# Three steps of a state-space layer's hand-written round moved to other places in the round

## The chip, the cores and the metric

The kernel runs on one core of a Trainium2 chip. A core has a matrix engine (TensorE, PE in the profile, with its weight loads shown apart as PEld), a vector engine (VectorE, DVE), an activation engine (ScalarE, ACT), a general engine (GpSimd, POOL) and DMA queues issued by SyncE (SP) and others. Each engine takes its own instructions in the order in which they stand in its queue, and waits on semaphores for the others. The metric is the device time of one execution in microseconds (us), lower is better; the median over several runs is compared.

## The reference

The whole kernel is a four-layer decoder stack of twelve sublayers on a tensor x of 32 sequences of 128 tokens with 128 features. Each sublayer is `x = x + f(layernorm(x))`. Only the first sublayer, a state-space layer, is touched here:

```
zxbcdt = x @ in_proj_w.T                 # z (256), xBC (512), dt (32)
xBC = silu(causal conv of width 4 over the tokens, + conv_b)
dt = 0.001 + 0.099 * sigmoid(dt_raw + dt_bias);  dA = dt * -exp(A_log)
Yd, Yo = products in chunks of 64 tokens, weighted by exp of sums of dA
y = (Yd + Yo + D_skip * x_ssm) * silu(z)
y = y * rsqrt(mean(y*y) + 1e-5) * norm_w
out = layernorm(y @ out_proj_w.T) * ln_w + ln_b
```

The result is added to the normalized input, and that sum to x.

## The kernel before

The 32 sequences are 8 groups (G = 8) of 4 sequences (J = 4). `layer0` walks through 34 rounds, n = -2 to 31; round n belongs to group i = n // 4 and to place j = n % 4 in it, and computes the chunk products of sequence j of group i. Around that core each round carries pieces of other groups' work, so that the engines have something to do while one product waits for the next. These pieces are generators: `go(what, g)` runs group g's next piece, up to its next `yield`. For TensorE, ScalarE and VectorE the order in which the program issues instructions is kept exactly (`follow(T, A, V)`, line 914; line 194 is the recording helper, so nearly every instruction bears that line in the profile). GpSimd's and SyncE's queues are ordered by the framework's scheduler.

The pieces that matter:

- `entry(g)`, line 753, the group's layer norm, four pieces. 1: statistics on VectorE and a power on GpSimd. 2: one small VectorE operation for the shift (`sh`, tile `s`). 3: four ScalarE activations that write `xn`. 4: GpSimd adds `xn` to x (line 758); TensorE transposes `xn` into a PSUM tile, and ScalarE copies that into `xnT`, which all projections of the group read.
- `decays(g)`, line 762, the step sizes, five pieces. 1: four small matmuls of `xnT` and a VectorE addition that writes `dts`. 2: a ScalarE tanh. 3: six VectorE operations, `dA` among them. 4: a matmul of `dA` (lines 784 and 785) and a ScalarE exponential. 5: one VectorE multiplication (line 788). The result is first read when `first` begins on that group's sequence 0.
- `gate(g, b)`, line 720, two pieces. 1: a matmul of `xnT`, a ScalarE copy to `z`, and a ScalarE tanh. 2: a VectorE operation on `z`.
- `conv(g, c)`, line 700, five pieces: projection and copy; the first tap on ScalarE (`gmid<-bmid,w`); three taps on VectorE; tanh; a VectorE product. One block c is done in each round, in the round's own group + 1 for j = 0 and 1, and + 2 for j = 2 and 3, so that round 2 is the first to read the newest `xnT`.
- `joined(g)`, line 864, the output: piece 1 is VectorE work (skip term, product with z); 2 two ScalarE squares; 3 the output projection `op`, a sum of squares `msp` and a ScalarE copy; 4 statistics, which read `msp` first; 5 two small VectorE operations; 6 four ScalarE activations; 7 GpSimd sums.
- `first(n)` prepares a sequence two rounds ahead (five matmuls, two transposes, three ScalarE reads of PSUM, three GpSimd products); `second`, `exponentials` and `weighted` make the decay weights one round ahead; `third(n)` does the 128 small matmuls of the chunk products and then two VectorE reads of PSUM (`gmid<-ps`).

All small PSUM tiles come from one pool of two buffers (`ps`, line 219). A tile can be written only when the readers of the tile before the last one are done. So the order of the steps also sets who waits for whose reader.

Of the kernel before, what the change touches and what calls it, by code (L numbers as in the profile page):

```python
# [204 lines left out]
def program(ctx, tc, cols, x, ctxt, mask, drop, dfirst, dsmall, dwide, drows, dunits, dexperts, dconst, drel, dwq, out):  # L205
# [466 lines left out]
    def layer0(lead):  # L672
# [119 lines left out]
        def first(n):  # L792

            i, j = n // J, n % J
            side, B, C = sides[i % 2], convs[i, 2], convs[i, 3]
            dt, dte = dts[i]
            xt, xd, xe, right = xts[n % 2], xds[n % 3], xes[n % 3], rights[n % 2]

            p = ps((128, 320))
            left, edge = (side[:, j, k].rearrange("p r c -> p (r c)") for k in range(2))  # L800
            mm(p[:, 256:320], edge, W0["fold64"])
            mm(p[:, 128:256], left, W0["upper64"])
            mm(p[:, 64:128], B[:, j, :], C[:, j, 64:128])
            for ch in range(2):
                at = slice(64 * ch, 64 * ch + 64)
                mm(p[at, 0:64], B[:, j, at], C[:, j, at])
            cbl = sm.tile([128, 384], F32, tag="cbl", name="cbl", bufs=CBLS)
            A.copy(cbl[:, 0:320], p)
            A.activation(cbl[:, 320:384], p[:, 256:320], AF.Exp)
            P.tensor_tensor(right, bc(cbl[:, 256:320], 1, 8), bc(W0["hm24"], 2, 64), ALU.mult)  # L810
            p = ps((128, 256))
            for c in range(2):
                turn_over(p[:, c * 128 : (c + 1) * 128], convs[i, c][:, j, :])
            A.copy(xt, p)
            P.tensor_tensor(diagonal(xd), xt.rearrange("p (a n e) -> p a n e", a=8, n=4),
                            bc(dt[:, j, :].rearrange("p (a n) -> p a n", a=8), 3, 8), ALU.mult)
            P.tensor_tensor(xe.rearrange("p (h e) -> p h e", e=8), xt[0:64].rearrange("p (h e) -> p h e", e=8),
                            bc(dte[0:64, j, :], 2, 8), ALU.mult)
            fronts[n] = xd, xe, cbl, right

        def second(n):

            _, _, cbl, right = fronts[n]
            segs = [two((128, 2, 8, 64)) for _ in range(2)]
            for r in range(4):
                mm(segs[r // 2][:, r % 2], identb, bc(acausal, 1, 8), True, False)
            for r in range(4):
                rows = slice(32 * r, 32 * r + 24)
                mm(segs[r // 2][:, r % 2], cbl[rows, 128:256], right[rows], False, True)
            mids[n] = bbig((128, 2, 16, 64)), segs  # L830

        def exponentials(n):
            m, segs = mids[n]
            for h in range(2):
                A.activation(m[:, h], segs[h].rearrange("p r a q -> p (r a) q"), AF.Exp)

        def weighted(n, h):

            m = mids[n][0]
            V.tensor_tensor(m[:, h], m[:, h], bc(fronts[n][2][:, 0:64], 1, 16), ALU.mult)  # L840

        def third(n):

            i, j = n // J, n % J
            (xd, xe, cbl, _), m = fronts.pop(n), mids.pop(n)[0].rearrange("p s h q -> p (s h) q")
            if j == 0:
                sums[i] = [acc((128, 2, J, 64)) for _ in range(2)]
                offs[i] = gmid((128, 2, J, 64))
            for b in range(2):
                for k in range(4):  # L850
                    for r in range(4):
                        for ch in range(2):
                            rows = slice(64 * ch, 64 * ch + 64)
                            mm(sums[i][ch][32 * r : 32 * r + 32, b, j], flat(xd[rows, 4 * b + r, k]), m[rows, 16 * b + 4 * r + k],
                               k == 0, k == 3)
            p = ps((128, 2, 2, 64))
            for b in range(2):
                mm(p[:, 0, b], xe[:, 128 * b : 128 * b + 128], cbl[0:64, 64:128])
            for b in range(2):
                mm(p[:, 1, b], K["spread"][:, 128 * b : 128 * b + 128], cbl[:, 320:384])  # L860
            V.tensor_copy(offs[i][:, :, j], p[:, 0])
            V.tensor_tensor(offs[i][:, :, j], offs[i][:, :, j], p[:, 1], ALU.mult)
# [43 lines left out]
        def go(what, g, *more):  # L906

            if 0 <= g < G:
                key = what, g, *more
                if key not in late:  # L910
                    late[key] = what(g, *more)
                next(late[key], None)
# [36 lines left out]
        for n in range(-2, G * J):  # L949
            i, j = n // J, n % J  # L950

            g, c = (i + 1, j) if j < 2 else (i + 2, j)
            go(conv, g, c)
            if 0 <= n + 2 < G * J:
                first(n + 2)
            go(conv, g, c)
            if j == 0:
                go(joined, i - 1)
                go(gate, i, 0)
            elif j == 1:  # L960
                go(joined, i - 1)
            elif j == 2:
                go(decays, i + 2)
                go(decays, i + 2)
            elif j == 3:
                go(decays, i + 2)
                go(gate, i + 1, 1)
                go(entry, i + 3)
            if 0 <= n + 1 < G * J:
                second(n + 1)  # L970
            go(conv, g, c)
            if 0 <= n + 1 < G * J:
                exponentials(n + 1)
                weighted(n + 1, 0)
            if 0 <= n < G * J:
                third(n)
            if 0 <= n + 1 < G * J:
                weighted(n + 1, 1)
            go(conv, g, c)
            if j == 0:  # L980
                go(joined, i - 1)
                go(joined, i - 1)
            elif j == 1:
                go(joined, i - 1)
                go(joined, i - 1)
                go(joined, i - 1)
                go(entry, i + 2)
            elif j == 2:
                go(decays, i + 2)
                go(decays, i + 2)  # L990
                go(gate, i + 1, 1)
            elif j == 3:
                go(entry, i + 3)
                go(entry, i + 3)
                go(gate, i + 1, 0)
            go(conv, g, c)
            if n >= G * J - 5:
                next(lead)
# [997 lines left out]
    SY.dma_start(out=wq8, in_=dwq)  # L1996
    lead1, run1 = layer1()
    rest0 = layer0(lead1)
    load_units(5)
    lead2, run2 = layer2()  # L2000
# [45 lines left out]
```

## Time and profile before

| | |
|---|---|
| median of 3 runs | 3010.7 us (3003.21, 3010.7, 3012.12) |
| the profiled execution | 2999.27 us, span 2997.5 us |
| share of the span: PE, PEld, DVE, ACT, POOL | 85%, 55%, 70%, 51%, 33% |
| the state-space layer | about the first 430 us of the span |
| steady group of four rounds (178.77 to 230.62) | 51.85 us, of them DVE busy 37.01, PE 41.49, ACT 26.88 |
| mean granted TensorE clock in that group | 0.84 of full |

A row of the timeline gives start and duration in us, the engine, the line, the operation with the tile written and the tiles read, and how many instructions were merged; in brackets stands how long the engine sat idle before it and which engine's work ended that idle time. A row of the waits gives the waiting engine and its tile, the releasing engine, the total us, the number of waits and the longest.

### The profile page before, as it was taken

How to read it: one execution, taken by the hardware profiler on the slowest of the kernel's cores; microseconds unless marked ns; L12 is line 12 of the kernel's file. 1: busy time of each engine (PE TensorE's matmuls, PEld its weight loads, DVE VectorE, ACT ScalarE, POOL GpSimd, SP SyncE). 2: the span in 40 equal slices, each digit the busy share in tenths (PEclk: the TensorE clock that was granted, in tenths of full speed). 3: DMA queues.
4: the chain of work that ended last, by engine and by line, in shares of the span. 5: the costliest groups of instructions: out<-in, count | busy, mean ns of one | idle time of the engine just before them, and what ended most of it. 6: DMA issues, size and time to landing. Idle time of an engine off the chain costs nothing. (4 is left out here: it accounts for less than half of the span.)

```text
span 2997.5 us, 55783 instructions
## 1 busy us (share of the span) xinstructions
PE 2554.4 (85%) x22535; PEld 1638.7 (55%) x22554; DVE 2093.0 (70%) x4263; ACT 1527.0 (51%) x3540; POOL 1003.2 (33%) x1033
## 2 busy tenths in 40 slices
PE   5788889999989989999998999988876989876564
PEld 3555567777744445566664444445553767544343
DVE  5777667888888756677786554468895339867873
ACT  4555445444412255666664444467772226555563
POOL 3333352232310123335451000124334365324544
PEclk8888889999999999999998999989997989997776
DMA  3000000000000000000000000000003253100000
GB/s 112 2 2 2 5 20 8 5 8 1 12 11 1 0 33 2 5 9 9 12 2 15 1 1 1 1 1 2 2 2 131 85 179 109 40 18 11 22 11 22
DMA packets 50147, 68.36 MB, mean 23 GB/s; under 512 B 3681, under 2 KB 41570, under 8 KB 49762
## 3 DMA queue, kind: packets, MB, share of 16 engines
q1 hardware_dynamic: 42608, 33.84, 3.7%
q0 software_dynamic: 6848, 27.81, 2.8%
q8 instruction: 178, 2.92, 0.4%
q10 hardware_dynamic: 434, 3.14, 0.3%
q14 instruction: 79, 0.65, 0.1%
HBM read 51.11 MB, written 13.68 MB: 22 GB/s over the span
## 5 line engine op out<-in xcount | busy, mean ns | idle before, releaser
L194 PE MATMUL ps<-cs,bbig 128*128 128x128 f32 x2208 | 328.5, 289 | 88.9 <-ACT bbig L194 34.9
L194 PEld LDWEIGHTS ps<-cs,bbig 128*128 128x128 f32 x2208 | 253.9, 146 | 192.4 <-ACT bbig L194 85.9
L194 ACT COPY bbig<-ps 128x512 f32<-128x512 f32 x418 | 228.9, 590 | 238.9 <-PE ps L194 238.9
L194 DVE TENSOR_REDUCE s<-two 128x8 f32<-128x1024 f32 (+1 forms) x192 | 234.1, 1220 | 119.6 <-PE two L194 118.3
L194 DVE TENSOR_TENSOR bbig<-bbig 128x256 f32<-128x256 f32 (+4 forms) x394 | 272.8, 742 | 18.6 <-ACT bbig L194 17.1
L194 PE MATMUL two<-xnT,u 128*128 128x512 f32 x512 | 260.8, 610 | 11.8 <-ACT bmid L194 6.3
L194 PE MATMUL acc<-bmid,u 128*128 128x512 f32 x448 | 239.4, 621 | 26.8 <-DVE bmid L194 25.2
L194 PE MATMUL two<-gbig,gmid 32*128 32x512 f32 (+1 forms) x1248 | 217.1, 570 | 2.4 <-ACT bbig L194 2.4
L194 DVE TENSOR_TENSOR bmid<-bmid,ps 128x512 f32<-128x512 f32 x192 | 130.2, 684 | 111.5 <-ACT bmid L194 91.8
L481 POOL TENSOR_SCALAR gbig<-bmid,cs 128x512 f32<-128x512 f32 x96 | 148.6, 1564 | 160.9 <-ACT bmid L194 160.9
L194 ACT ACTIVATE bbig<-two,s 128x256 f32<-128x256 f32 (+1 forms) x512 | 189.7, 419 | 20.2 <-DVE s L194 16.8
L194 ACT ACTIVATE bbig<-bbig 128x512 f32<-128x512 f32 (+1 forms) x160 | 128.1, 801 | 87.0 <-DVE bbig L194 86.6
L194 PE MATMUL ps<-cs,xn 128*128 128x128 f32 x288 | 68.9, 321 | 105.8 <-ACT xn L194 80.5
L194 ACT ACTIVATE bmid<-two 128x512 f32<-128x512 f32 x104 | 62.0, 597 | 190.5 <-PE two L194 182.1
L194 PEld LDWEIGHTS two<-xnT,u 128*128 128x128 f32 x512 | 92.2, 192 | 115.7 <-issue 55.8
L194 PEld LDWEIGHTS acc<-bmid,u 128*128 128x128 f32 x448 | 81.9, 197 | 128.9 <-DVE bmid L194 73.2
L194 ACT ACTIVATE bmid<-two,ws 128x512 f32<-128x512 f32 x128 | 85.1, 686 | 112.1 <-PE two L194 111.9
L194 ACT ACTIVATE bbig<-bbig,s 128x128 f32<-128x128 f32 x384 | 118.7, 387 | 27.1 <-DVE s L194 27.1
L1070 POOL TENSOR_TENSOR bbig<-bbig,s 128x1024 f32<-128x1024 f32 x32 | 60.6, 1892 | 214.1 <-PE two L194 152.6
L194 DVE TENSOR_TENSOR bbig<-two,s 128x1024 f32<-128x1024 f32 (+1 forms) x128 | 122.6, 958 | 8.6
L493 POOL MEMSET val<- 128x512 f32 x72 | 39.3, 549 | 257.3 <-PE acc L194 256.1
L194 PE MATMUL two<-xT,we 128*128 128x256 f32 x448 | 109.8, 400 | 8.6 <-ACT xT L194 4.2
(307 smaller groups left out, 5930.6 us busy)
## 6 DMA issues: line engine op xcount, KB each, us to landing
u<-in_units SPq DMA_DIRECT2D x10, 768.0 KB, 4.3
gmid<-in_ctx SPq DMA_DIRECT2D x16, 256.0 KB, 2.9
xs<-bbig SPq DMA_DIRECT2D x4, 903.0 KB, 5.7
xt<-xs SPq DMA_DIRECT2D x28, 129.0 KB, 2.3
x<-in_x SPq DMA_DIRECT2D x8, 256.0 KB, 7.2
gmid<-in_mask SPq DMA_DIRECT2D x8, 256.0 KB, 3.1
ys<-bbig SPq DMA_DIRECT2D x2, 1024.0 KB, 6.2
gmid<-ys SPq DMA_DIRECT2D x8, 256.0 KB, 3.9
```

What stands on the lines that cost most here:

```text
L194: d = f(*args, **kwargs)
L481: P.tensor_scalar(o[:, n, :], k, K["n4"][:, n : n + 1], None, ALU.mult)
L493: P.memset(o, 0.0)
L1070: (V if c2 else P).tensor_tensor(pr[:, four, :], pr[:, four, :], bc(nm[:, four], 2, 256), ALU.mult)
```

## The change

Three things move in the rounds; no operation is added or removed.

- The fourth piece of the norm, `entry(i + 2)` with the transposes, goes from the end of round j = 1 to the end of round j = 0.
- The fourth and fifth piece of `decays` each go later: the fourth (matmul of `dA`, exponential) from the end of round 2 to the end of round 3, the fifth (the multiplication) from the start of round 3 to the start of the next group's round 0, where it stands ahead of the first piece of `joined`.
- At the end of round 3, `gate(i + 1, 0)` goes ahead of the second and third piece of `entry(i + 3)`, and the moved piece of `decays` stands behind all of them.

```
             if j == 0:
+                go(decays, i + 1)
                 go(joined, i - 1)
                 go(gate, i, 0)
...
             elif j == 3:
-                go(decays, i + 2)
                 go(gate, i + 1, 1)
                 go(entry, i + 3)
...
             if j == 0:
                 go(joined, i - 1)
                 go(joined, i - 1)
+                go(entry, i + 2)
             elif j == 1:
                 go(joined, i - 1)
                 go(joined, i - 1)
                 go(joined, i - 1)
-                go(entry, i + 2)
             elif j == 2:
-                go(decays, i + 2)
                 go(decays, i + 2)
                 go(gate, i + 1, 1)
             elif j == 3:
+                go(gate, i + 1, 0)
                 go(entry, i + 3)
                 go(entry, i + 3)
-                go(gate, i + 1, 0)
+                go(decays, i + 2)
             go(conv, g, c)
```

In the built program GpSimd's and SyncE's instructions stand in the same order as before; those of TensorE, ScalarE and VectorE are moved as the diff says.

More of the change, by code (lines that the diff above doesn't have):

```diff
@@ L957, in layer0 @@
             if j == 0:
+                go(decays, i + 1)
                 go(joined, i - 1)
@@ L965, in layer0 @@
             elif j == 3:
-                go(decays, i + 2)
                 go(gate, i + 1, 1)
@@ L982, in layer0 @@
                 go(joined, i - 1)
+                go(entry, i + 2)
             elif j == 1:
@@ L986, in layer0 @@
                 go(joined, i - 1)
-                go(entry, i + 2)
             elif j == 2:
-                go(decays, i + 2)
                 go(decays, i + 2)
@@ L992, in layer0 @@
             elif j == 3:
+                go(gate, i + 1, 0)
                 go(entry, i + 3)
                 go(entry, i + 3)
-                go(gate, i + 1, 0)
+                go(decays, i + 2)
             go(conv, g, c)
```

## The prediction, made before the changed kernel was run

> **What bounds the kernel now.** I read the busy shares first (no engine is full in the first 430 us, where the changed layer runs), then the waits between 30 and 372 us, then the timeline of one group. The waits show which hand-overs cost VectorE and TensorE time:
>
> ```profile
> DVE dts L194 <- PE ps L194: 41.6, 7, 7.9
> ...
> PE ps L194 <- ACT xnT L194: 22.3, 5, 4.6
> PE ps L194 <- DVE dA L194: 21.7, 8, 4.2
> ...
> DVE z L194 <- ACT bmid L194: 14.7, 8, 2.4
> ACT xn L194 <- DVE s L194: 12.5, 6, 2.2
> ```
>
> All five touch moved steps. In the group that I take as the pattern (i = 3) they stand so:
>
> ```profile
> 222.95 1.65 ACT L194 ACTIVATE bmid<-bmid,s 128x128 f32<-128x128 f32 x4 [2.38 <-DVE s L194]
> 224.51 0.56 ACT L194 COPY xnT<-ps 128x512 f32<-128x512 f32 x1
> ...
> 225.12 2.08 PE L194 MATMUL ps<-xnT,w 128*128 128x512 f32 x2 [4.63 <-ACT xnT L194]
> ...
> 227.23 0.58 ACT L194 COPY bmid<-ps 128x512 f32<-128x512 f32 x1 [2.16 <-PE ps L194]
> ...
> 228.83 0.43 ACT L194 COPY cbl<-ps 128x320 f32<-128x320 f32 x1 [1.01 <-PE ps L194]
> ...
> 230.62 0.29 DVE L194 TENSOR_TENSOR dts<-ps,ww 128x128 f32<-128x128 f32 x1 [7.10 <-PE ps L194]
> ...
> 236.74 0.22 DVE L194 TENSOR_SCALAR dts<-dts 128x128 f32<-128x128 f32 x1
> ...
> 237.43 0.66 PE L194 MATMUL ps<-dA,w 64*64 64x128 f32 x2 [2.40 <-DVE dA L194]
> ...
> 241.41 0.69 DVE L194 SCALAR_TENSOR_TENSOR z<-bmid,z 128x512 f32<-128x512 f32 x1 [2.44 <-ACT bmid L194]
> ...
> 244.89 2.92 DVE L194 SCALAR_TENSOR_TENSOR gmid<-bmid,w,gmid 128x508 f32<-128x508 f32 x3 [1.53 <-ACT gmid L194]
> ```
>
> Round 2 begins with a chain: ScalarE's `joined` activations, then the `xnT` copy, then TensorE's projection, ScalarE's copies, the step-size matmuls; VectorE sits 7.10 us until `dts`. Round 3 has another: TensorE stands 2.40 us at `dA`, with the gate's and the convolution's matmuls behind it, so the gate's `z` comes late for VectorE (2.44) and then the convolution's taps (1.53). The end of round 3 and the start of round 0 read differently:
>
> ```profile
> 199.05 0.69 DVE L194 SCALAR_TENSOR_TENSOR gmid<-bmid,gmid 128x512 f32<-128x512 f32 x1
> 199.17 1.65 ACT L194 ACTIVATE xn<-x,s 128x128 f32<-128x128 f32 x4 [2.18 <-DVE s L194]
> 199.65 1.65 DVE L194 SCALAR_TENSOR_TENSOR bmid<-gmid,w,acc 128x256 f32<-128x256 f32 x4
> 200.72 0.56 ACT L194 COPY z<-ps 128x512 f32<-128x512 f32 x1
> ```
>
> From 199.65 to 213.0 VectorE has no gap: round 0 is VectorE's.
>
> **The norm's transposes, a round sooner.** Round 2: `xnT` is ready, so the projection follows `third` at 220.0 instead of 225.12. The step that ends last is then ScalarE's: its four `joined` activations still end at 224.60 (they wait for VectorE's `s`). Its copy follows at once, 224.6 to 225.2, and the `cbl` copy at 225.2 instead of 228.83. From there the old spacing holds (step sizes on VectorE 1.8 us after the `cbl` copy): 227.0 instead of 230.62, 3.6 us. Against that, VectorE's taps now fall under GpSimd's sums of `joined` (224.68 to 227.28) and its products; such taps took 2.92 to 3.10 us where 2.54 stood here, so 3.2 are left. Groups 1 to 5 have this; group 0, with no `joined` before it, waited 2.22 instead of 7.10 and gains 1.2. Sum 1.2 + 5 x 3.2 = 17.2.
>
> TensorE still has one idle stretch there: `first`'s transposes need the PSUM buffer that ScalarE's copy frees at 225.2, and all before them is done by 222.4, so 2.8 us. The row for such a stretch is the matmul of `dA`: after 2.40 us it took 0.66 (half rate) in groups -1, 3 and 5 and 0.40 in four others. [...] By the row it is three times in seven, and the price then is that of group 5, where the step-size matmuls took 1.92 instead of 1.08 us: with the transposes 1.1 us on the path. The rule gives 17.2, all cold 11.7; I go by the row: 3/7 x 1.1 x 5 = 2.4 less, 15.
>
> Round 0, where the transposes go: four matmuls, 0.61 us, behind `msp`, and ScalarE's 0.56 us copy. Round 1's projection stands behind them (its buffer was `msp`'s), and with it `first`, the taps and VectorE, which already waits 1.60 us for the taps there. So 0.65 us of loss in six groups, 3.9. GpSimd's addition at line 758 keeps its place, and no DMA moves.
>
> **The products of the step sizes, a round later.** Round 3: TensorE is done with round 2's `third` at 235.04 and goes straight to the gate (1.1 us), ScalarE's copy and tanh of `z` follow by 237.4, the convolution's projection at 236.2, its copy at 237.4, and the tap on ScalarE ends 3.2 us after VectorE's step-size operations begin. VectorE itself needs from their start 2.06 us to the gate's product and 2.1 us for that and the statistics: its taps can start at 4.16 us. Before, they started after 7.69, 7.11, 5.57, 7.00, 8.15, 5.57 and 7.12 us (groups -1 to 5; the last has no statistics, so 3.2 after). Sum 48.2 - (6 x 4.16 + 3.2) = 20.0 if TensorE runs at full rate; at half rate the gate's and the convolution's matmuls take 2.0 instead of 1.1 each and `first` 0.8 more, so the taps start at about 5.5 everywhere, and 48.2 - 38.5 = 9.7 is the gain. Three sevenths of the way from the first: 15.6.
>
> **The same products, where they go.** The `dA` matmul finds its buffer free when VectorE has read `third`'s tile, a wait (0.47 us) that round 0's projection has today. Then the exponential stands behind the norm's four activations (end 200.82): 201.1. `first`'s matmuls, behind it by the buffer, start at 201.15 instead of 201.34. But VectorE's multiplication now stands at the head of round 0, ahead of `joined`, and cannot start before 201.1; queued behind it are all of round 0's VectorE operations, and for these wait ScalarE's squares and TensorE's `msp`. `joined` starts at 201.4 instead of 199.65: 1.75 us, the multiplication's 0.28 included. Part may come back, because GpSimd's two sums (200.89 to 203.57) then run beside the four operations that read PSUM and not beside those with two SBUF inputs. [...] That gives back up to 1.0, so 0.75. I take 1.3 between the two. If TensorE is at half rate, the gate's matmul takes 2.0, the norm's activations slip to 199.85, and it is 2.4. It counts where `joined` and a norm meet, groups 1 to 5: 6.5 (3.75 to 12).
>
> **The gate ahead of the norm.** ScalarE copies and squashes `z` in the 2.18 us that it waits for `s` (1.2 us of work, matmul done at 197.6), so nothing. Without that cover it would delay `xn`, which is the 2.4 above.
>
> **The sum.** 15 + 15.6 - 3.9 - 6.5 = 20 us. Worst ends together: 11.7 + 9.7 - 3.9 - 12 = 5.5; best: 17.2 + 20.0 - 3.9 - 3.75 = 29.5. What follows the layer is in the same queues and starts that much sooner. Against the profiled execution, 2999.3 (span 2997.5 and 1.8 around it), this is 2979. The median shown stands 11.4 above it; I subtract from the median: 3010.7 - 20 = 2991 (2981 to 3005).
>
> **The rivals.** A: the VectorE wait at the head of round 0 takes back most of what rounds 2 and 3 give, with TensorE at half rate: the worst ends, 3005. For it: three of seven `dA` rows were at half rate. Against: it needs all of them.
>
> B, slower: the half rate spreads. Round 2 took 6.12 us from `dts` to the step-size operations at full rate, 8.64 in group 5 and 7.58 in group 2; round 3's taps came 2.6 us later cold. So a cold round costs about 2.5 us, and it was cold in seven of the thirteen such rounds. The change cuts TensorE's stretches into other lengths, and one of 2 to 3 us stays in each group. From eight more cold rounds among the 28 the 20 us are gone; sixteen more give 3010.7 - 20 + 40 = 3031. Against: the longest stretch, 4.63 us, is removed, and the mean clock should rise.
>
> C: the waits are exchanged without gain, since something else ends each group, within 9 us: 3006. Against: VectorE is busy 37.01 of 51.85 us, and the gaps removed are its own.
>
> **Chances.** Forecast 0.70, A 0.13 (0.04 of it still a gain above 0.3%), B 0.12, C 0.05. A measurement of this kernel tells about 0.3%, 9 us, from no change. Faster 0.70 + 0.04 = 0.74, same 0.09 + 0.05 = 0.14, slower 0.12. The range runs from the best end, 2980, to 3014, leaving out B and a little below.
>
> **What would show it.** In the changed profile the wait of PE for `xnT` is gone (it was 22.3), DVE's for `dts` falls from 41.6 to about 22 (5 x 3.6 + 1.2 less), PE's for `dA` from 21.7 to near the prologue's 4; DVE's for `z` vanishes; a new wait of DVE for ACT `dts`, about 1.4 us each in five groups, appears, and PE waits for `xnT` again at most briefly, in round 1. A steady group takes about 47.5 instead of 51.5 us. I am wrong if a group's granted clock falls under 0.8, or if the new wait is above 5 us.

## The result, and the profile after

| | before | changed |
|---|---|---|
| median of 12 runs each | 3010.64 us (3003.21 to 3025.06) | 2985.33 us (2978.25 to 3006.37) |
| ratio of the two | | 0.9925, 95% interval 0.9906 to 0.9944 |
| the profiled execution, its span | 2999.27, 2997.5 us | 2981.45, 2979.7 us |
| start of `joined` in groups 1 to 6 | 97.7 to 354.7 us | 97.3 to 334.6 us |
| the group i = 3: length, TensorE's granted clock | 51.55 us, 0.83 | 47.64 us, 0.86 |

The changed kernel is faster, by 22.6 us if the ratio is taken of 3010.64, and by 17.8 between the two profiled executions. In the traces the layer alone gives 20.1 us by the start of group 6's `joined`; 2.3 us of that are lost again by the end of the span. The twelve executions of the changed kernel differ in TensorE's granted clock: over the whole span it was 0.924 in the fastest (2978.25 us), and 0.915, 0.914 and 0.912 in the three slowest (2992.62, 3000.57 and 3006.37 us).

The waits between 30 and 360 us of the changed kernel (total us, number of waits and longest):

```profile
DVE dts L194 <- PE ps L194: 22.8, 7, 4.1
...
PE ps L194 <- ACT bmid L194: 20.6, 12, 3.0
...
PE ps L194 <- DVE gmid L194: 15.5, 14, 1.9
...
PE ps L194 <- ACT dts L194: 8.2, 6, 1.5
...
DVE dts L194 <- ACT dts L194: 7.6, 6, 1.3
...
ACT xn L194 <- DVE s L194: 5.7, 6, 1.0
...
PE ps L194 <- DVE dA L194: 4.2, 1, 4.2
```

VectorE's wait for `dts` is halved (it was 41.6). TensorE's for `dA` (21.7) is down to the prologue's one, TensorE's for `xnT` (22.3) and VectorE's for `z` (14.7) are not in the list any more. In their place TensorE waits for ScalarE's `bmid` copy (20.6, where it was 8.9), and VectorE for ScalarE's `dts` at the head of round 0 (7.6).

Round 2 of group i = 3 in the timeline of the changed kernel (start, duration, engine, operation, and in brackets the idle time before it):

```profile
215.75 1.65 ACT L194 ACTIVATE bmid<-bmid,s 128x128 f32<-128x128 f32 x4 [2.38 <-DVE s L194]
217.31 0.56 ACT L194 COPY bmid<-ps 128x512 f32<-128x512 f32 x1
...
217.77 0.42 ACT L194 COPY cbl<-ps 128x320 f32<-128x320 f32 x1
...
217.92 0.44 PE L194 MATMUL ps<-cs,gmid 128*128 128x128 f32 x2 [2.35 <-ACT bmid L194]
...
218.36 1.88 PE L194 MATMUL ps<-w,xnT 128*128 128x32 f32 x8
...
220.34 0.29 DVE L194 TENSOR_TENSOR dts<-ps,ww 128x128 f32<-128x128 f32 x1 [4.02 <-PE ps L194]
...
220.55 3.14 DVE L194 SCALAR_TENSOR_TENSOR gmid<-bmid,w,gmid 128x508 f32<-128x508 f32 x3
```

VectorE's wait for `dts` is 4.02 us where it was 7.10. TensorE's idle stretch before `first`'s transposes is 2.35 us, and the step-size matmuls behind it take 1.88 us: the half rate. The end of round 3 and the head of round 0:

```profile
237.44 0.40 PE L194 MATMUL ps<-dA,w 64*64 64x128 f32 x2 [1.86 <-DVE gmid L194]
...
238.54 1.65 ACT L194 ACTIVATE xn<-x,s 128x128 f32<-128x128 f32 x4 [1.04 <-DVE s L194]
240.10 0.26 ACT L194 ACTIVATE dts<-ps 64x128 f32<-64x128 f32 x1
...
240.27 1.27 POOL L758 TENSOR_TENSOR x<-x,xn 128x512 f32<-128x512 f32 x1 [5.30 <-ACT xn L194]
240.38 1.30 DVE L194 TENSOR_TENSOR dts<-dts 64x128 f32<-64x128 f32 x1 [1.27 <-ACT dts L194]
...
241.61 1.64 DVE L194 SCALAR_TENSOR_TENSOR bmid<-gmid,w,acc 128x256 f32<-128x256 f32 x4
```

The new wait is 1.27 us, and the multiplication behind it takes 1.30 us beside GpSimd's addition (L758), where it took 0.28 before.

To see where the 20 us came from, I cut each group at VectorE's own marks: the start of `joined`, round 0's taps, the reading of `msp`, round 1's taps, the `dts` addition, `dA`, round 3's taps, the next `joined`. Sums over groups 1 to 5, from the timelines, in us:

| from, to | before | changed | gain |
|---|---|---|---|
| `joined` to round 0's taps | 38.23 | 28.93 | 9.3 |
| round 0's taps over `msp` to round 1's taps | 48.47 | 53.77 | -5.3 |
| round 1's taps to `dts` | 70.90 | 52.31 | 18.6 |
| `dts` to `dA` | 35.84 | 42.02 | -6.2 |
| `dA` to round 3's taps | 32.15 | 20.74 | 11.4 |
| round 3's taps to the next `joined` | 31.46 | 39.49 | -8.0 |
| sum | 257.05 | 237.26 | 19.8 |

### The profile page after: what moved, and what is told of

It reads as the page before. It is cut to its first block, busy times and chain, and to the rows that moved or that the text cites. A ratio compares the mean times of both kernels' runs of the same rounds, so it can differ in the third digit from the quotient of the medians.

```text
span 2979.7 us, 55782 instructions
## 1 busy us (share of the span) xinstructions
PE 2551.2 (86%) x22535; PEld 1632.4 (55%) x22554; DVE 2095.4 (70%) x4263; ACT 1525.5 (51%) x3540; POOL 1008.7 (34%) x1033
## 5 line engine op out<-in xcount | busy, mean ns | idle before, releaser
L194 PE MATMUL two<-xT,we 128*128 128x256 f32 x448 | 108.3, 396 | 10.7 <-DMA we<-in_experts,wrow 5.9
```

Source lines behind the costliest of these rows:

```text
L194: d = f(*args, **kwargs)
```

## The experiments

The theory is that of the prediction: three separate chains, each with its own gain, whose sum is the result. The rivals are that the wait at the head of round 0 takes back a large part (A), and that TensorE's half rate decides (B). Runs sent together share a chip and the runs of the kernel before; ratios are to the kernel before on the same chip, with 95% intervals. "Step" below is 3.413 us, the grid on which TensorE's granted clock changes in these traces; the last section shows it.

**Each part alone, on the kernel before.** The norm's transposes alone:

```diff
             if j == 0:
...
                 go(joined, i - 1)
+                go(entry, i + 2)
             elif j == 1:
...
-                go(entry, i + 2)
```

> The kernel before, with the norm's transposes alone moved a round sooner. The sum on record has this at 15.0 - 3.9 = 11 us faster (about 3000). The reading of the changed trace says otherwise: round 2 starts its step sizes 3.2 us sooner, but the wait of 2.35 us before the two transposes puts TensorE at half rate, so that the step-size operations come 8.2 instead of 6.1 us after it, and round 1 loses 0.5: 5 x (3.2 - 2.2 - 0.5) + about 1 = 3 to 4 us faster at most, within 9 us of before. A group's stretch from dts to the step-size operations shows which: 6.1 us or 8.2 us.

Measured: 0.9979 (0.9965 to 0.9992), 6 us. Round 2's gain is there (round 1's taps to `dts` 10.7 us instead of 13.86), but `dts` to `dA` takes 8.5 instead of 6.37, `dA` to round 3's taps takes 7.9 to 8.0 in every group, and all groups are 50.9 to 51.1 us long.

The products of the step sizes alone:

```diff
             if j == 0:
+                go(decays, i + 1)
                 go(joined, i - 1)
...
             elif j == 3:
-                go(decays, i + 2)
...
             elif j == 2:
-                go(decays, i + 2)
                 go(decays, i + 2)
...
                 go(gate, i + 1, 0)
+                go(decays, i + 2)
```

> The kernel before, with pieces 4 and 5 of the step sizes alone moved later. The sum on record: 15.6 - 6.5 = 9 us faster. The reading of the changed trace: the taps of round 3 start 4.65 us after the step-size operations in every group (48.2 - 7 x 4.65 = 15.7 us sooner), and VectorE's new wait at the head of round 0 is paid back by less overlap with GpSimd: 14 to 17 us faster, about 2995. With the gate still behind the norm's activations, the exponential comes about 1.2 us later than in the full change, and VectorE's wait at the head of round 0 is about 2.5 us instead of 1.27.

Measured: 0.9969 (0.9955 to 0.9982), 9 us. `dA` to round 3's taps is 4.40 as in the changed kernel, and the head of round 0 gives back nearly all that its wait costs (`joined` to taps 5.13 instead of 7.65, taps to `joined` 8.37 instead of 6.31). But `dts` to `dA` is 7.8, and four of five groups are 51.2 to 52.4 us long: what round 3 gave, other rounds lost.

The gate alone:

```diff
             elif j == 3:
+                go(gate, i + 1, 0)
                 go(entry, i + 3)
                 go(entry, i + 3)
-                go(gate, i + 1, 0)
```

> The kernel before, with the gate's piece alone moved ahead of the norm's pieces at the end of round 3. Both theories: ScalarE does it while it waits for the norm's shift; first's matmuls of round 0 come about 2 us sooner on TensorE, but VectorE sets the end of round 0, so no difference (within 5 us of before). A rival: TensorE's wait of 2.17 us in front of round 0 is what puts it at half rate there, and without it round 0 runs at full rate, 1 us per group, 5 us faster.

Measured: 1.0074 (1.0059 to 1.0089), 22 us slower. This was expected by neither theory. The groups are 56.3 to 57.3 us long. The matmuls of that kernel that write `msp`, and the projection behind them (timeline, TensorE):

```profile
167.58 2.40 PE L194 MATMUL ps<-cs,bmid 128*128 128x1 f32 x16 [3.17 <-ACT bmid L194]
169.84 2.05 PE L194 MATMUL ps<-xnT,w 128*128 128x512 f32 x2
```

The projection behind the wait takes 2.05 us, the half rate, where it takes 1.08 at full rate, and round 1's taps start 5.24 us after `msp` instead of 3.41. Here I changed my theory: the parts are not separate. What they seem to share is TensorE's clock, so that B's mechanism would be at work although B's outcome is not.

**Is it the wait in front that sets the half rate?** I filled it, with the gate alone, by matmuls into tiles that are overwritten afterwards. The first try placed 14 in the tile of `msp`:

```diff
-            op, msp = ps((128, J, 128)), ps((128, J))
+            op, wide = ps((128, J, 128)), ps((128, 512))
+            msp = wide[:, 0:J]
...
+            if g < G - 1:
+                for _ in range(14):
+                    mm(wide[:, 128:512], identb, bc(acausal, 1, 6), True, True)
```

> The kernel with the gate alone moved (22 us slower than before), with 14 matmuls of no use (bf16, 384 columns, overwritten columns of the msp tile, about 2.7 us at full rate) in TensorE's wait of 3.17 us in front of msp. If the slowness is TensorE's half rate after that wait, these matmuls keep the full rate, joined's head to dts comes back to the 31 us of the kernel before from 34.5, and groups take about 51 instead of 56.4 us: ratio 0.998 to 1.003 instead of 1.0074. If the slowness is in the order of the waits itself, the extra matmuls change nothing or cost up to 2.7 us in six groups: ratio 1.0074 to 1.013.

Measured: 1.0099 (1.0077 to 1.0122). It was ill placed: the fillers needed the same buffer and stood behind the same wait (3.08 us), so they ran after it and not in it. Round 1 was at full rate behind them in three of the five groups (3.41 us from `msp` to the taps again; 5.24 in the two others), yet the groups took 54.8 to 59.9 us. The second try put ten into `op`'s tile, ahead of `op`:

```diff
             op, msp = ps((128, J, 128)), ps((128, J))
+            if g < G - 1:
+                for _ in range(10):
+                    mm(flat(op), identb, bc(acausal, 1, 8), True, True)
```

> The kernel with the gate alone moved, with ten bf16 matmuls of no use (128x512, about 2.5 us at full rate) into op's PSUM tile ahead of op's own matmuls, which overwrite them. The fillers before stood behind the wait for msp's buffer and ran after it; these run before it, so that TensorE's 3.17 us in front of msp shrink to under 1. If the half rate after that stretch is what makes the gate alone slow, rounds 0 and 1 run at full rate (msp to the taps of round 1 in 3.4 instead of 5.2 us), a group takes 51 to 53 us instead of 56.4, and the ratio is 0.998 to 1.003. If the half rate comes all the same later in the group, the ratio stays at 1.005 to 1.010.

Measured: 1.006 (1.0038 to 1.0082), so still slower than before. The timeline shows that this time the fill is in the right place:

```profile
163.83 2.32 PE L194 MATMUL ps<-acausal,identb 128*128 128x512 bf16 x10
...
169.09 1.92 PE L194 MATMUL ps<-cs,bmid 128*128 128x1 f32 x16 [1.15 <-ACT bmid L194]
171.26 1.47 PE L194 MATMUL ps<-xnT,w 128*128 128x512 f32 x2 [0.25 <-DVE s L194]
```

The wait is 1.15 us instead of 3.17, and the projection still changes to half rate in its middle (1.47). So either a wait of 1.15 us is enough, or something other than the wait sets the rate. This run does not decide between the two.

**The head of round 0.** The multiplication moved behind the first piece of `joined`, in the changed kernel, so that the new wait stands in nobody's way (rival A would see its price come back):

```diff
             if j == 0:
-                go(decays, i + 1)
                 go(joined, i - 1)
+                go(decays, i + 1)
```

> The changed kernel, with the product of the step sizes (piece 5) behind the first piece of joined instead of ahead of it, so that VectorE no longer waits for the exponential at the head of round 0. If that wait is a pure loss, as the sum on record took it for the most part (1.3 of 1.75 us in 5 groups), this is 6 to 9 us faster than the changed kernel. If it only moves the overlap with GpSimd's two sums, as the changed trace suggests (joined's head to its taps 5.79 instead of 7.65 us), it is within 3 us of the changed kernel.

Measured: 0.9934 (0.9914 to 0.9955), as the changed kernel's 0.9925. The new wait costs nothing that a move could give back, which speaks against A. The trace shows why. In groups 1 to 5 VectorE does not wait for the exponential any more; `joined` starts 6.31 us after round 3's taps, as in the kernel before, and lies under GpSimd's sums again:

```profile
191.10 1.65 DVE L194 SCALAR_TENSOR_TENSOR bmid<-gmid,w,acc 128x256 f32<-128x256 f32 x4
...
192.34 1.27 POOL L758 TENSOR_TENSOR x<-x,xn 128x512 f32<-128x512 f32 x1 [4.53 <-ACT xn L194]
...
193.92 1.64 DVE L194 TENSOR_TENSOR bmid<-bmid,z 128x512 f32<-128x512 f32 x1
```

From round 3's taps over `joined` to round 0's taps VectorE takes 14.15 us here, 14.06 in the changed kernel with its wait of 1.27 us, and 13.51 with the step sizes alone, where that wait is 2.40 us. The later `joined` starts, the less its operations are slowed beside GpSimd: the product in the last row takes 1.00 us in the changed kernel, and 0.69 with the step sizes alone. The profiled execution (3016.78 us) was the longest of its runs and had groups of 51.2 us at a granted clock of 0.73; the kernel's runs spread from 2986.54 to 3016.78.

**The chain of round 2, shortened further.** In the changed kernel `first`'s transposes wait until ScalarE is done with `joined`'s four activations. Here the last two pieces of `joined` go behind `first`, into round 2:

```diff
             elif j == 2:
+                go(joined, i - 1)
+                go(joined, i - 1)
                 go(decays, i + 2)
...
                 go(joined, i - 1)
-                go(joined, i - 1)
-                go(joined, i - 1)
             elif j == 2:
```

> The changed kernel, with pieces 6 and 7 of joined moved from the end of round 1 to round 2, behind first. The copy that frees the PSUM buffer for first's transposes then no longer stands behind ScalarE's four joined activations, and TensorE's wait of 2.35 us in round 2 goes. If that wait is what puts the rest of round 2 at half rate, the stretch from VectorE's dts to its step-size operations falls from 8.4 to 6.1 us, dts itself comes up to 3 us sooner, and a group takes 43 to 45 us instead of 47.6: 12 to 22 us faster than the changed kernel, ratio about 0.986 to the kernel before. If the half rate has another cause, dts comes sooner but the stretch stays at 8.4: 5 to 12 us faster. If TensorE only waits longer elsewhere and turns to half rate there, no gain.

Measured: 0.9879 (0.9861 to 0.9897), some 36 us under the kernel before (2969.74 against 3005.84): this version beats both. Its timeline (TensorE):

```profile
208.59 0.98 PE L194 MATMUL ps<-w,xnT 128*128 128x32 f32 x8
209.41 1.71 PE L194 MATMUL two<-acausal,identb 128*128 128x512 bf16 x4
211.05 2.09 PE L194 MATMUL two<-gbig,cbl 24*128 24x512 f32 x8
```

`dts` comes 7.9 us after round 1's taps (10.65 in the changed kernel). TensorE's longest waits around it are 0.56 and 0.54 us, and the half rate comes all the same, from about 209.5 on: the 128x512 matmuls take 1.71 instead of 1.03 us. From `dts` to `dA` it still takes 8.0 us. The groups at 186.0 and 230.3 are 44.3 us long; the three others are 45.1, 46.8 and 41.2.

The same wait, filled with useful work: the next sequence's four mask matmuls ahead of `first`'s transposes in round 2.

```diff
-        def first(n):
+        def first(n, between=None):
...
+            if between is not None:
+                between()
             p = ps((128, 256))
...
-                first(n + 2)
+                first(n + 2, (lambda: masks(n + 1)) if j == 2 and n > 0 else None)
```

> The changed kernel, with the four mask matmuls of second moved into TensorE's wait of 2.35 us in round 2, ahead of first's transposes (1.03 us at full rate). The wait falls to about 1.3 us. If an idle stretch of that length keeps the full rate, the step-size matmuls take 1.08 instead of 1.88, and dts to the step-size operations falls from 8.4 to about 5.5 (6.1 less the masks, which are done): 8 to 14 us faster than the changed kernel, ratio about 0.989. If the half rate comes all the same, only the masks' 1.9 us at half rate are saved in each of five groups less what they cost before: 3 to 8 us.

Measured: 0.9908 (0.9884 to 0.9932), between the changed kernel and the last. The step-size matmuls are at full rate (1.08 us), and `dts` to `dA` is 6.95 instead of 8.60. But in the two groups from 184.6 on the half rate stands elsewhere (round 0's taps to `msp` 8.5 instead of 6.05 us), and these take 47.6 us where the first two took 45.2.

**Pairs.** One part at a time taken out of the changed kernel. Without the gate:

```diff
             elif j == 3:
-                go(gate, i + 1, 0)
                 go(entry, i + 3)
                 go(entry, i + 3)
+                go(gate, i + 1, 0)
                 go(decays, i + 2)
```

> The changed kernel without the gate's move: the norm's transposes and the step sizes alone. If the parts add up (alone they gave -6, -9 and +22 us), this is 15 us faster than before, ratio 0.995, and if the gate hurts in this company too, it is faster than the changed kernel. If the gate's harm needs the missing wait of round 0 (in the changed kernel first waits for the exponential there instead), the gate does nothing in this company: ratio 0.992 to 0.993, as the changed kernel.

Measured: 0.9936, with steady groups of 47.6 us as in the changed kernel; its interval, 0.9911 to 0.9961, holds both of the expected ratios.

Without the norm's step:

```diff
                 go(joined, i - 1)
-                go(entry, i + 2)
             elif j == 1:
...
                 go(joined, i - 1)
+                go(entry, i + 2)
             elif j == 2:
```

> The changed kernel without the norm's move: step sizes and gate. If the parts add up: 13 us slower than before, ratio 1.004. If the exponential's wait takes the place of the one that the gate removed, the gate does no harm: ratio 0.996 to 0.998, as the step sizes alone.

Measured: 0.9973, as the step sizes alone. The sum of the parts, 1.004, lies outside the interval.

Without the step sizes' (shown against the kernel before):

```diff
                 go(joined, i - 1)
+                go(entry, i + 2)
             elif j == 1:
...
-                go(entry, i + 2)
...
             elif j == 3:
+                go(gate, i + 1, 0)
                 go(entry, i + 3)
                 go(entry, i + 3)
-                go(gate, i + 1, 0)
```

> The changed kernel without the step sizes' move: norm and gate. Here nothing takes the place of the wait in round 0, so TensorE is early for msp and waits there; both ways of counting say slower than before: ratio 1.004 to 1.008, with groups of 54 to 56 us.

Measured: 1.0031, slower than before, if a little less than expected, with groups of 54.3 to 54.6 us.

All eight combinations together; the length is that of the steady groups, without the first and the last, which are often shorter or longer:

| parts | ratio | group, us | in steps |
|---|---|---|---|
| none (all groups) | 1 | 48.96 to 54.55 | uneven |
| norm | 0.9979 | 51.1 | 15 |
| step sizes | 0.9969 | 51.2, one 52.4 | 15 |
| gate | 1.0074 | 56.3 to 56.4 | 16.5 |
| norm, step sizes | 0.9936 (0.9911 to 0.9961) | 47.6 | 14 |
| step sizes, gate | 0.9973 (0.9959 to 0.9988) | 51.2 | 15 |
| norm, gate | 1.0031 (1.0013 to 1.005) | 54.6 | 16 |
| all three | 0.9925 | 47.6 | 14 |

The parts do not add. The gate costs 22 us alone, some 16 beside the norm's step, and nothing that can be measured beside the step sizes' step. The two others together give about what they give one by one added up (0.64% against 0.21 and 0.31%). And the steady lengths are not spread over all values: but for one group they lie within 0.3 us of whole (once a half) multiples of 3.413 us. In some kernels one can watch them approach: with norm and gate the groups take 54.33, 54.55, 54.58 and 54.60 us, where 16 steps are 54.61.

**Is the length really locked?** If so, a little work added to the changed kernel can cost more than itself, up to a whole step. One product of VectorE, 0.69 us, with no effect on what comes after it but its time (the maximum of z and z):

```diff
             V.scalar_tensor_tensor(z, t, 1.0, z, ALU.add, ALU.mult)
+            if b == 0:
+                V.scalar_tensor_tensor(z, z, 0.0, z, ALU.add, ALU.max)
```

> The changed kernel with one VectorE product of 0.69 us more in round 0 of each group (the larger of z + 0 and z, which is z), in the stretch where VectorE has no gap. If engine waits alone set the length of a group, it grows from 47.6 to 48.3 us. If the group is held to the 3.41 us grid on which TensorE's half-rate stretches begin and end (27.3, 20.5, 27.3, 20.5 us from start to start in the changed kernel, so 8 + 6 = 14 steps of 3.413 = 47.8), the added time is taken up by a shorter piece of half-rate work, and groups take 47.8, or the pattern jumps to 15 steps, 51.2; 48.3 does not last over several groups.

Measured: 0.9955 (0.9939 to 0.9971), 9 us dearer than the changed kernel by the two ratios and 11.7 by the two traces over groups 1 to 5, where the added work is 0.69 us a group, 3.5 in all. The intervals of the ratios overlap (their difference is 2 to 17 us, an estimate from both widths), so the times alone do not rule out 3.5; the step rests on the one trace. There two of the five groups (192.9 and 244.1) are 51.2 us long, 15 steps; the others are 48.2, 49.6 and 48.8. In the group at 192.9 the product itself costs 0.73 us; the rest, 2.8 us, stands where TensorE is at half rate: round 0's taps to `msp` 7.72 instead of 6.05, `dts` to `dA` 9.65 instead of 8.60. Stretches of that kernel (columns: window, its length, busy us of PE, PEld, DVE, ACT and POOL with their instructions, then granted clock, DMA share and GB/s):

```profile
192.90:244.10 51.20, 46.26 (x701) 30.63 (x699) 37.74 (x76) 26.88 (x50) 19.83 (x19) 0.73 0.01 2
191.50:205.10 13.60, 13.41 (x175) 9.94 (x176) 13.23 (x19) 5.84 (x11) 5.51 (x5) 0.50 0.01 2
205.10:218.80 13.70, 11.23 (x197) 7.88 (x195) 8.19 (x23) 7.58 (x15) 4.66 (x6) 1.00 0.00 1
218.80:232.40 13.60, 13.16 (x162) 8.04 (x163) 7.31 (x14) 5.79 (x11) 5.58 (x5) 0.50 0.01 2
```

And of the changed kernel:

```profile
194.00:241.60 47.60, 40.48 (x700) 26.08 (x699) 36.98 (x75) 26.53 (x50) 20.11 (x19) 0.86 0.01 2
218.40:225.30 6.90, 6.90 (x124) 4.01 (x127) 3.52 (x5) 2.70 (x5) 4.67 (x5) 0.51 0.01 2
238.90:245.70 6.80, 5.30 (x25) 3.04 (x24) 5.49 (x9) 3.56 (x10) 5.33 (x5) 0.50 0.00 0
245.70:266.20 20.50, 16.82 (x358) 12.39 (x350) 15.44 (x33) 12.01 (x23) 5.91 (x7) 1.00 0.01 2
266.20:273.10 6.90, 6.90 (x147) 4.01 (x147) 3.97 (x5) 2.89 (x5) 4.50 (x5) 0.51 0.01 4
```

In the changed kernel a steady group holds two half-rate stretches of two steps each (218.4, 238.9, 266.2, ...); the product makes each of them four steps long. The same TensorE work (700 and 701 matmuls) takes 40.48 us in the one and 46.26 in the other.

## Why the prediction was right, and which of its terms were not

The direction, the mechanism of the large gains and the time (2991 forecast, 2985.33 measured; 2979 forecast and 2981.45 measured for the profiled execution) came out. The sum is better than its parts: several terms were wrong and cancelled, so that it came out at 20 us almost exactly is in part luck.

- **Round 2, the wait for `dts`: right.** 3.6 us sooner in each of five groups, 18; measured 18.6. TensorE's wait for `xnT` is gone, and VectorE's for `dts` fell to 22.8 (forecast about 22). The one idle stretch that was to be left, 2.8 us, is there with 2.35.
- **Round 2, the half rate: weighed too low.** I took it in three groups of seven, by the row of `dA`. It stands in all five, in the last of them only behind the step-size matmuls (these take 1.88, 1.91, 1.88, 1.73 and 1.08 us; 1.08 is full rate). The end of 17.2 in the forecast lets an idle stretch of 2.8 us cost nothing. No run shows that; the trace of the changed kernel has the half rate behind 2.32 to 2.35 us. The loss in `dts` to `dA`, 6.2 us, is 1.8 above the forecast's 4.4 (2.4 for the half rate and 0.4 x 5 for the slower taps). It is not more because two of the five groups of before had paid already (7.84 and 8.89 us).
- **Round 3: right in size.** My way of weighing gives 10.3 of the 15.6 to groups 1 to 5; measured 11.4. At that place TensorE is at full rate in all of them, and the taps start 4.4 us after `dA`, that is 4.65 after the first step-size operation, where 4.16 was forecast for full rate.
- **Round 1: too low.** 0.65 x 5 = 3.25 forecast, 5.3 measured. The norm's step alone lengthens `msp` to the taps from 3.41 to 3.88, 0.47 a group; the rest stands in the groups at 97.3 and 289.1, where they are 5.47 and 5.98.
- **The head of round 0: the step that failed.** 1.3 x 5 = 6.5 of loss was forecast; measured is a gain of 1.3. In the group i = 3 `joined` starts 1.96 us later after round 3's taps (8.27 against 6.31; I had said 1.75), and the taps then come 1.86 us sooner after it (5.79 against 7.65). I had let GpSimd's sums give back up to 1.0; no run shows that term, and in its place the runs showed 1.84, the difference of the five operations below (6.24 us before, 4.40 after). Two things were mis-sized: the multiplication takes 1.30 us instead of 0.28, because it stands beside GpSimd's addition itself, and all that VectorE does afterwards is the freer for it (the four operations that read PSUM take 1.64 us beside GpSimd's second sum, where they took 1.65; the five operations behind the first of `joined` took 1.23, 1.64, 1.26, 1.00 and 1.11 us before; after 241.61 they take 1.17, 1.00, 0.85, 0.69 and 0.69). The kernel with the product behind the first piece bears GpSimd's overlap out as the reason: there `joined` starts at its old place against GpSimd's addition, 1.24 us ahead of it as in the kernel before, its operations take 1.22, 1.64, 1.26 and 1.00 us again, and nothing is gained by the missing wait.
- **Groups -1 and 0: 5.8 us forecast, 0.3 measured.** The 5.8 is 1.2 of round 2 and 5.3 of round 3, less 0.65. In the changed kernel TensorE is at half rate for 17.1 us, from 51.2 to 68.3, where in the same window of the kernel before the granted clock is 0.90; round 1's taps wait 3.15 us there.
- **The gate: nothing forecast, and beside the two others nothing that can be measured** (0.9936 without it, 0.9925 with it, with intervals that overlap). The argument for it, ScalarE's cover, was not the whole: alone on the kernel before it costs 22 us. That is cost that I had not looked for, since I worked out each move in the company of the other two.

Summed over groups 1 to 5 the forecast was 14.2 and the result 19.8; 5.8 and 0.3 for the first two groups bring both to 20. Rival A is refuted: the wait is there, at the size named (1.27 against about 1.4), and is paid back (14.06 us over that stretch with it, 14.15 without). Rival C is refuted by the gain. Rival B's outcome did not come, but its mechanism, the half rate moving to other rounds, is what goes with the length of the groups in every kernel that was measured. The mark that I set for being wrong, a group's granted clock under 0.8, was not met by the changed kernel's trace (0.86), but by the profiled execution of the kernel with the product behind the first piece (0.73). The changed kernel's own spread, 28 us between its runs, is as wide. Its slowest runs had the lowest granted clock, 0.912 against 0.924; groups of 15 steps would account for that, but only one of its executions has a trace that would show them.

What stays open: what decides about the half rate. The filled waits tested only the wait in front. Neither the idle time nor the busy share of a stretch separates the cases; the last section has the numbers.

## What to carry to other kernels

A step-wise sum of waits gave this change its sign, but its parts could not have been sold singly: in a loop whose TensorE alternates between two rates, take the group's length after each edit, in multiples of the step that its traces show (3.413 us here), and ask which stretches run at half rate, before ascribing a gain to the edit. The busy time of the profile does not answer that: here TensorE was busy for 13.41 of 13.60 us at a granted clock of 0.50. A small edit can then be worth nothing or a whole step (with 0.69 us of work more, two of five groups were 51.2 us long where 47.6 stood), so edits have to be tried in company, and one that loses alone may be free beside another (the gate's 22 us). A wait on an engine that competes with GpSimd may cost nothing, if the work behind it afterwards runs with less overlap (14.06 us with the wait of 1.27, 14.15 without).

## What the runs showed of the hardware

The granted clock of TensorE has two values in these traces, and within one execution it changes on a fixed grid. In windows of 0.5 us from 30 to 360 us, nine of the traces have it at 0.50 or 1.00 in every window but those in which it changes (628 of 660 in the changed kernel). In the changed kernel the half-rate stretches begin at 191.1, 218.4, 238.9, 266.2 and 286.7 us: 27.3, 20.5, 27.3 and 20.5 apart, which is 8, 6, 8 and 6 times 3.413; together 14 steps, 47.8, beside groups of 47.5 to 47.6. In the nine traces the stretches that begin after 33 us last 1 to 5 whole steps, 3.4 to 17.1 us. What I had not expected is the consequence. In these kernels the group's length settles at or just under a multiple of the step: 44.3 us with `joined`'s activations later (two groups; 13 steps are 44.4), 47.6 (14, 47.8), 51.2 (15), 54.6 (16), while the kernel before has irregular stretches (beginning at 99.7, 120.2, 147.5, 171.4, 188.4, ...) and uneven groups. Not all groups do: with the masks moved, three were 45.2 to 45.4 us long, and first and last groups are often between two multiples.

Neither waits nor busy time, as the profile shows them, tell when the half rate comes. It came behind a wait of 2.35 us in the changed kernel, and with none longer than 0.56 us around it in the kernel with `joined`'s activations later. In the kernel with one product more TensorE was busy for 13.41 of 13.60 us, four steps, and stayed at 0.50; in the changed kernel it was busy for 16.82 of 20.50 us, six steps, at 1.00. Busy in the profile is the span of its matmuls, with modelled ends. What the clock follows is not shown by these runs.
